# Loading the expert blocks of a routed FFN block by block instead of four at a time

## The chip, the core and the metric

The kernel runs on one core of one Trainium2 chip. The metric is the device time of one execution in microseconds. Six executions of the kernel before gave a median of 1012.49 us (1010.12 to 1017.5). One execution was profiled; its own time is 1010.9 us, and the span of the trace is 1009.1 us. Times below are microseconds from the start of that span.

## What is computed

The input is 64 sequences of 128 tokens of width 128, and a context of 77 keys of width 96 for each sequence. The reference, cut to its two steps:

```python
x = x + xattn(layernorm(x), ctx, w_q, w_kv, w_out, b_out)       # 16 heads of 64
x = x + ffn(layernorm(x), router_w, w1, w2, w3, sw1, sw2, sw3)  # 8 experts, each token goes to 2
...
for e in range(8):                     # the routed part; hidden width 176
    h = silu(x2 @ w1[e].T) * (x2 @ w3[e].T)
    moe_out = moe_out + gate[:, e:e+1] * (h @ w2[e].T)
```

A shared expert (sw1, sw2, sw3) is added for every token. The reference computes all experts for all tokens and multiplies by a gate that is zero for six of the eight; the kernel computes only the two chosen ones, except for the last tokens.

## The kernel before, in words

**Work and its order.** The 64 sequences are 16 groups of 4 (512 tokens each). The attention runs in 128 units, two for each sequence. A unit has two half slots, so the program has 256 half slots, numbered 0 to 255. Everything that is not attention is hung into half slots by hand: `at(when, step)` puts a step into the table `plan`, and `run(when)` (L979) issues the steps of one half slot in the order in which they were put there. At the end of the kernel function all instructions of one engine are tied to their program order, so every engine, and SP that issues most DMAs, works strictly in the order in which the steps were issued. There are no priorities.

**Sets and blocks.** The first 15 groups are routed in three sets of 7, 5 and 3 groups (`SETS`). For each group a router picks two experts for each token, and POOL scatters the normalised rows by indirect DMA into a DRAM buffer `sent` of the set (`send`, L587), ordered by expert. When a set is complete, `tables` (L675) counts the rows of every expert on DVE, reads eight end positions into SP's registers (`values`, L666), writes eight DMAs of filler rows (L691), and works out for each block of 128 rows where its rows begin and which expert's weights it needs. A block is 128 rows of one expert. Four blocks make a `Quad` (L725); the sets have 16, 12 and 8 quads. `Set.ready` is the half slot from which a set's quads can run: 127, 207 and 255.

**A quad's steps.** `load` (L731) reads eight table entries into SP's registers, then issues for each of the four blocks a DMA of its rows (`xb`, L740, 65 KB) and one of its packed weights (`w`, L748, 312 KB): eight DMAs, 1.5 MB. `transpose` (L751) turns the four blocks on TensorE, with a copy on ACT. `first` and `rest` are the up projections (L761) and the gate on ACT and DVE, `down` (L769) the down projection, and `answer` (L783) scatters the result by indirect DMA on POOL. A quad of the first two sets with its transposes in half slot p has `load` at p-3, `first` at p+1, `rest` at p+2 and `down` at p+4 (L900 to L909). In the first set p grows by 5 from quad to quad, in the second by 4. `xb` has 4 buffers of a whole quad; `w` has 12 buffers of one block each, so a block's weights can be loaded once the block 12 before has had its `down`.

**What else SP issues in order.** The inputs of later groups (L105, L107, L112), the attention's last values `vo` (L378, one for each sequence, right after the even half slot 4m; it waits for a buffer that the output product of two sequences before frees), the parked residuals (L616), and for the first set's results `Combine` (L795): loads of parked rows and answers (L804, L805) in half slots 211 to 223, and stores (L816) in half slots 215 to 227. A store waits for DVE's two additions (L812), which are issued one half slot earlier.

**The ending.** After half slot 255 `ending` (L957) runs a list of jobs, one pass of its loop each: the last set's quads b0 to b7 (program names 2_0 to 2_7), a shared expert, and the eight dense experts e0 to e7 for the sixteenth group. The order is b0 b1 b2 shared b3 e0 b4 e1 b5 e2 b6 e3 b7 e4 e5 e6 e7. Pass k issues: the load of job k+2; the steps of `combining` for the second set's results; `first` of job k; the transposes of job k+1; `rest` of job k; `down` and the answers of job k-1. In `combining`, passes 2 to 6 load one group's results each through POOL's queue (2 to 6 issue groups 0 to 4), and passes 4 to 8 add them on DVE (L812) and store them through SP (L816); the last set's results follow in the same way after b7. A dense expert's load is one DMA of weights (L634). The loads of b0 and b1 are issued in half slots 253 and 254, before the loop.

Of the kernel before, what the change touches and what calls it, by code (L numbers as in the profile page):

```python
# [8 lines left out]
F32 = mybir.dt.float32  # L9
# [15 lines left out]
E, I = 8, 176  # L25
# [9 lines left out]
QUAD = 4  # L35
# [15 lines left out]
DW = D + 2  # L51
# [6 lines left out]
def xattn_moe_kernel(  # L58
# [28 lines left out]
    ffn = ctx.enter_context(tc.tile_pool(name="ffn", bufs=2))  # L87
# [59 lines left out]
    rows = most * T + 128  # L147
# [57 lines left out]
    def bank(name, p=128):  # L205
        return ps_g.tile([128, 512], F32, tag="g", name=name)[:p]
# [37 lines left out]
    class Norm:  # L244


        def __init__(self, name, src):
            self.name, self.src = name, src
# [39 lines left out]
    class Attention:  # L288
# [66 lines left out]
        def values(self, b):  # L355

            vo = self.vo[b]
            for t in range(2):

                pv = bank(f"pv_{self.g}_{b}_{t}")  # L360
                for r in range(4):
                    odd, half = divmod(r, 2)
                    nc.tensor.matmul(  # L363
                        pv[r * 32 : (r + 1) * 32],
                        self.cT[:, b, 32 * half : 32 * (half + 1)],
                        wvo_sb[:, 8 * t + odd : 8 * (t + 1) : 2, :],
                        start=True,
                        stop=True,
                    )
                nc.scalar.copy(vo[:, 4 * t : 4 * (t + 1), :], pv.rearrange("p (m d) -> p m d", d=D))  # L370
# [247 lines left out]
    class Dense(Router):  # L618
# [13 lines left out]
        def load(self, e):  # L632
            self.w[e] = ffn.tile([128, WALL], F32, tag="w", name=f"w_d{e}", bufs=3 * QUAD)
            nc.sync.dma_start(out=self.w[e], in_=wx[e * 128 : (e + 1) * 128, :])  # L634
# [90 lines left out]
    class Quad:  # L725
# [2 lines left out]
        def __init__(self, st, q):  # L728
            self.st, self.q, self.name = st, q, f"{st.i}_{q}"

        def load(self):  # L731
            st = self.st
            self.w = []
            self.xb = ffn.tile([128, QUAD, DW], F32, tag="xb", name=f"xb_{self.name}", bufs=4)
            first = slice(QUAD * self.q, QUAD * (self.q + 1))
            froms = values(st.from_row[0:1, first], E * rows)
            wrows = values(st.w_row[0:1, first], (E - 1) * 128)
            for j in range(QUAD):
                w = ffn.tile([128, WALL], F32, tag="w", name=f"w_{self.name}_{j}", bufs=3 * QUAD)
                ins = nc.sync.dma_start(out=self.xb[:, j, :], in_=sent[st.i][bass.ds(froms[j], 128), :])  # L740
                for other in st.scatters:
                    tc.add_manual_dep(
                        ins.ins,
                        other.ins.name,
                        mybir.DependencyInfo(mybir.DependencyClass.Sync, mybir.DependencyReason.DATA),
                        reason="rows of this block",
                    )
                nc.sync.dma_start(out=w, in_=wx[bass.ds(wrows[j], 128), :])  # L748
                self.w.append(w)
# [73 lines left out]
    def at(when, *steps):  # L823
        plan.setdefault(when, []).extend(steps)
# [30 lines left out]
    for g in range(NG):  # L855
        p = 16 * g
# [11 lines left out]
    def route(g, step, *args):  # L868
        if g not in routers:
            st = next((s for s in sets if s.start <= g < s.start + s.n), None)  # L870
            routers[g] = (Router if st else Dense)(g, st, atts[g].x1)
        getattr(routers[g], step)(*args)
# [10 lines left out]
    for g in range(NG - 1):  # L883
        p = 16 * (g + 1)
        routing(g, p, (0, "stats"), (1, "normed"), (2, "transpose"), (3, "logits"), (4, "choose"), (5, "choose_second"))
    for st in sets:
        for g in range(st.start, st.start + st.n):
            p = 16 * (g + 1)
# [7 lines left out]
    end = 16 * NG  # L896

    for st, after in zip(sets, sets[1:]):
        until = after.ready - 4
        for q in range(st.quads):  # L900
            quad = Quad(st, q)
            p = st.ready + (until - st.ready) * q // (st.quads - 1)
            at(p - 3, quad.load)
            at(p, quad.transpose)
            at(p + 1, quad.first)
            at(p + 2, quad.rest)
            at(p + 4, quad.down)
            for j in range(QUAD):
                at(p + 5 + j // 2, lambda quad=quad, j=j: quad.answer(j))  # L909
        if after is not sets[-1]:  # L910
            for j in range(st.n):
                c = Combine(st, j, nc.sync)
                at(p + 8 + 2 * j, c.load)
                at(p + 11 + 2 * j, c.add)
                at(p + 12 + 2 * j, c.store)

    class Job:


        def __init__(self, of=None, **steps):  # L920
            self.steps = {k: getattr(of, k) for k in ("load", "transpose", "first", "rest", "down") if hasattr(of, k)}
            self.steps.update(steps)
            if of is not None:
                self.steps["answer"] = lambda: [of.answer(j) for j in range(QUAD)]

        def do(self, step):
# [11 lines left out]
    jobs = blocks[:3] + [shared]  # L938
# [18 lines left out]
    def ending():  # L957
        for k in range(max(len(jobs) + 2, max(combining) + 1)):
            job = jobs[k] if k < len(jobs) else Job()
            for step in ahead_of.get(k, ()):  # L960
                route(NG - 1, step)
            if k + 2 < len(jobs):
                jobs[k + 2].do("load")
            for step in combining.get(k, ()):
                step()
            job.do("first")
            if k + 1 < len(jobs):
                jobs[k + 1].do("transpose")
            job.do("rest")
            if 0 < k <= len(jobs):  # L970
                jobs[k - 1].do("down")
                jobs[k - 1].do("answer")

    at(end - 3, lambda: jobs[0].do("load"))
    at(end - 2, lambda: jobs[1].do("load"))
    at(end - 1, lambda: jobs[0].do("transpose"))
    at(end + 4, ending)

    def run(when):  # L979
# [124 lines left out]
```

## Time and profile before

| | |
|---|---|
| median of 6 runs | 1012.49 us |
| the profiled execution: time, span | 1010.9 us, 1009.1 us |
| TensorE (PE) | 967.0 us busy, 96%; mean granted clock 0.989 |
| VectorE (DVE) | 681.5 us, 68% |
| ScalarE (ACT) | 532.1 us, 53% |
| GpSimd (POOL) | 505.8 us, 50% |
| SP's DMA queue | 93.91 MB, its packets 30.6% of 16 engines' span |
| weights of blocks (L748) | 144 DMAs of 312 KB |
| rows of blocks (L740) | 144 DMAs of 65 KB |

How to read it. The page has for each engine its busy time, and in 40 slices how busy each was, the clock that was granted to TensorE and how busy the 16 DMA engines were. The view of waits adds up for each engine what ended its idle times. The view of windows gives the busy time of every engine, the granted clock and the DMA engines' share in stretches that the reader chooses; a share near 1 says that the transfers themselves are the limit there. The timeline of one engine lists its instructions in order with start and length; for SP these are the issues of DMAs, each about 0.33 us, not the transfers. When a transfer landed is recorded by the DMA engines' updates of its semaphore; the chain of work shows such a transfer as one piece from its issue to its landing.

### The profile page before, as it was taken

The page shows a single profiled execution, that of the slowest core. Times are in us where ns is not written, and L with a number is a line of the kernel's source. Part 1 is how long each engine was busy: PE and PEld are TensorE (multiplying, and loading weights), DVE is VectorE, ACT ScalarE, POOL GpSimd, SP SyncE. Part 2 cuts the span into 40 slices and gives each one's busy share as a digit, 9 for nine tenths or more (in the row PEclk, how much of TensorE's full clock was granted, in tenths as well). Part 3 has the DMA queues.
Part 4 walks back from the last instruction along what each step waited for, and adds up shares of the span by engine and source line. Part 5 has one row for each costly group of instructions (what it writes and reads, how often), then busy time and mean ns, then how long its engine had stood idle before and what let it go on. Part 6 is the DMA issues. An engine that isn't in the chain of part 4 may idle for free.

```text
span 1009.1 us, 19581 instructions
## 1 busy us (share of the span) xinstructions
PE 967.0 (96%) x6475; PEld 722.7 (72%) x6475; DVE 681.5 (68%) x1758; ACT 532.1 (53%) x1217; POOL 505.8 (50%) x629
## 2 busy tenths in 40 slices
PE   7999999999999997999999999999999999899896
PEld 5666667666666665768778777776777878778684
DVE  4565666677666766667656666667777866766877
ACT  4555555554646463655556565564654655445341
POOL 3334544536263625355474664646547566465542
PEclk9999999999999998999999999999999999999998
DMA  4212111211111214554343551352758575257964
GB/s 150 76 42 72 52 40 50 75 43 44 57 64 39 68 43 136 169 158 134 105 138 113 159 177 63 126 166 62 226 177 292 180 226 173 84 158 239 354 207 146
DMA packets 98372, 128.26 MB, mean 127 GB/s; under 512 B 13152, under 2 KB 62560, under 8 KB 98272
## 3 DMA queue, kind: packets, MB, share of 16 engines
q1 hardware_dynamic: 82704, 93.91, 30.6%
q0 software_dynamic: 10240, 23.73, 6.9%
q10 hardware_dynamic: 5328, 9.37, 2.5%
q8 instruction: 52, 0.85, 0.3%
q14 instruction: 48, 0.39, 0.1%
HBM read 91.23 MB, written 35.74 MB: 126 GB/s over the span
## 4 chain that ended last, share of the span: by engine, by line
PE 78%; DVE 9%; ACT 5%; DMA 3%; issue 3%; POOL 2%; ACTq 0%; DVEq 0%; SPq 0%; POOLq 0%
PE py L398 13%; PE pk L308 12%; PE ps L324 10%; PE pv L363 10%; PE p L761 5%; PE pa L388 5%; PE pq L773 3%; PE pq L774 3%; PE pn L408 3%; PE ph L761 2%; PE p_s L598 2%; PE pf L611 2%; PE pl L497 1%; PE pf L610 1%; PE pt L754 1%
## 5 line engine op out<-in xcount | busy, mean ns | idle before, releaser
L351 POOL TENSOR_TENSOR at<-sc,ri 128x512 f32<-128x512 f32 x128 | 134.6, 1052 | 267.0 <-DVE ri L348 159.0
L785 POOL DMA_INDIRECT answers<-y,to x144 | 142.2, 988 | 92.4 <-ACT y L781 37.3
L315 ACT COPY kx<-pk 128x308 f32<-128x308 f32 x256 | 100.2, 426 | 146.3 <-PE pk L308 140.1
L324 PE MATMUL ps<-kx,xgT 128*128 128x308 f32 x512 | 158.4, 431 | 10.7 <-DVE sc L335 5.8
L398 PEld LDWEIGHTS py<-vo,aT 128*128 128x128 f32 x1280 | 155.6, 195 | 12.3 <-ACT vo L370 3.8
L398 PE MATMUL py<-vo,aT 128*128 128x128 f32 x1280 | 156.6, 279 | 2.1 <-ACT vo L370 2.0
L308 PE MATMUL pk<-cT,wkq_sb 96*128 96x308 f32 x512 | 156.3, 429 | 1.0 <-DVE wkq_sb L229 1.0
L587 POOL DMA_INDIRECT sent<-pay,row x120 | 118.2, 985 | 71.3 <-DVE part L577 39.6
L339 ACT ACTIVATE sc<-sc,rs_a 128x616 f32<-128x616 f32 x128 | 105.0, 820 | 70.9 <-DVE sc L335 60.7
L346 DVE TENSOR_REDUCE sm<-sc 128x8 f32<-128x616 f32 x128 | 101.3, 791 | 50.0 <-ACT sc L339 48.4
L391 ACT COPY aT<-pa 128x512 f32<-128x512 f32 (+1 forms) x256 | 96.3, 430 | 61.4 <-PE pa L388 54.7
L363 PE MATMUL pv<-wvo_sb,cT 96*32 96x512 f32 x1024 | 123.2, 599 | 0.0
L308 PEld LDWEIGHTS pk<-cT,wkq_sb 96*128 96x128 f32 x512 | 88.8, 190 | 47.8 <-ACT aT L391 15.1
L324 PEld LDWEIGHTS ps<-kx,xgT 128*128 128x128 f32 x512 | 89.6, 191 | 46.0 <-PE pv L363 9.1
L333 DVE TENSOR_REDUCE mx<-ps 128x8 f32<-128x616 f32 x128 | 98.6, 770 | 22.0 <-PE ps L324 21.0
L335 DVE TENSOR_TENSOR sc<-ps,mx 128x616 f32<-128x616 f32 x128 | 102.3, 800 | 12.9 <-DVE mx L333 1.0
L388 PE MATMUL pa<-ident,at 128*128 128x128 f32 x640 | 91.0, 273 | 1.4 <-POOL at L351 1.3
L388 PEld LDWEIGHTS pa<-ident,at 128*128 128x128 f32 x640 | 75.7, 141 | 22.3 <-issue 11.8
L761 PEld LDWEIGHTS p<-xT,w 128*128 128x128 f32 x576 | 68.4, 192 | 9.9 <-ACT xT L756 4.0
L761 PE MATMUL p<-xT,w 128*128 128x128 f32 x576 | 71.1, 277 | 2.6 <-ACT xT L756 2.6
L370 ACT COPY vo<-pv 128x512 f32<-128x512 f32 x128 | 69.6, 587 | 1.3 <-PE pv L363 0.7
L363 PEld LDWEIGHTS pv<-wvo_sb,cT 96*32 96x32 f32 x1024 | 26.8, 109 | 48.9 <-issue 39.8
(154 smaller groups left out, 1405.8 us busy)
## 6 DMA issues: line engine op xcount, KB each, us to landing
w<-in_wx_dram SPq DMA_DIRECT2D x144, 312.0 KB
xb<-sent SPq DMA_DIRECT2D x144, 65.0 KB
last_values<-vn ACTq DMA_DIRECT2D x32, 256.0 KB
vo<-last_values SPq DMA_DIRECT2D x64, 128.0 KB
xg<-in_x_dram SPq DMA_DIRECT2D x16, 256.0 KB
xgT<-in_xT_dram SPq DMA_DIRECT2D x16, 256.0 KB
ya<-answers POOLq DMA_DIRECT2D x8, 512.0 KB, 5.9
parked<-x SPq DMA_DIRECT2D x15, 256.0 KB
```

The costliest lines, as they stand in the source:

```text
L308: nc.tensor.matmul(pk[:, :TK].rearrange("p (b k) -> p b k", k=NKV), wkq_sb[:, h, :], self.cT[:, :, :NKV], start=True, stop=True,)
L324: nc.tensor.matmul(ps[:, r, : 4 * NKV].rearrange("p (j k) -> p j k", k=NKV), self.xgT[:, ts], self.kx[:, h : h + 4, ks], start=True, stop= ...
L335: nc.vector.tensor_tensor(at, sc, over_keys(mx), ALU.subtract)
L339: nc.scalar.activation(at, at, AF.Exp, scale=self.norm.rs[:, b : b + 1])
L346: nc.vector.tensor_reduce(sm, at, AX.X, ALU.add)
L351: nc.gpsimd.tensor_tensor(main, at[:, :, :, :KM], over_keys(ri, KM), ALU.mult)
L363: nc.tensor.matmul(pv[r * 32 : (r + 1) * 32], self.cT[:, b, 32 * half : 32 * (half + 1)], wvo_sb[:, 8 * t + odd : 8 * (t + 1) : 2, :], sta ...
L388: nc.tensor.transpose(pa[:, j * NQ : (j + 1) * NQ], keys[:, c : c + 128], ident)
L398: nc.tensor.matmul(py[:, :D], aT[:, m, :], vo[:, m, :], start=(m == 0), stop=(m == NT - 1))
L587: ins = nc.gpsimd.indirect_dma_start(out=sent[st.i], out_offset=bass.IndirectOffsetOnAxis(ap=self.row[:, i : i + 1], axis=0), in_=self.pay ...
L761: nc.tensor.matmul(to[:m, ts], self.w[j][:, c : c + m], self.xT[:, ts], start=True, stop=True)
L785: ins = nc.gpsimd.indirect_dma_start(out=answers[st.i], out_offset=bass.IndirectOffsetOnAxis(ap=self.to[:, j : j + 1], axis=0), in_=self.y ...
```

## The change

`load` takes the numbers of the blocks that it is to load. The registers and the `xb` buffer are set up with block 0. In the first two sets block j is loaded in half slot p-5+j, but not before `ready`-3. In the ending a pass issues blocks 0 and 1 of job k+2 where it issued the whole load, and blocks 2 and 3 after `rest`, before the `down` of job k-1. The loads of b0 and b1 come in four half slots from 252 to 255.

```diff
-        def load(self):
+        def load(self, *js):
             st = self.st
-            self.w = []
-            self.xb = ffn.tile([128, QUAD, DW], F32, tag="xb", name=f"xb_{self.name}", bufs=4)
-            first = slice(QUAD * self.q, QUAD * (self.q + 1))
-            froms = values(st.from_row[0:1, first], E * rows)
-            wrows = values(st.w_row[0:1, first], (E - 1) * 128)
-            for j in range(QUAD):
+            if 0 in js:
+                self.xb = ffn.tile([128, QUAD, DW], F32, tag="xb", name=f"xb_{self.name}", bufs=4)
+                first = slice(QUAD * self.q, QUAD * (self.q + 1))
+                self.rows = values(st.from_row[0:1, first], E * rows), values(st.w_row[0:1, first], (E - 1) * 128)
+                self.w = []
+            froms, wrows = self.rows
+            for j in js:
...
             p = st.ready + (until - st.ready) * q // (st.quads - 1)
-            at(p - 3, quad.load)
+            for j in range(QUAD):
+                at(max(st.ready - 3, p - 5 + j), lambda quad=quad, j=j: quad.load(j))
             at(p, quad.transpose)
...
-            self.steps = {k: getattr(of, k) for k in ("load", "transpose", "first", "rest", "down") if hasattr(of, k)}
+            self.steps = {k: getattr(of, k) for k in ("transpose", "first", "rest", "down") if hasattr(of, k)}
             self.steps.update(steps)
             if of is not None:
+                self.steps["load"] = lambda: of.load(0, 1)
+                self.steps["load_more"] = lambda: of.load(2, 3)
...
             job.do("rest")
+            if k + 2 < len(jobs):
+                jobs[k + 2].do("load_more")
             if 0 < k <= len(jobs):
                 jobs[k - 1].do("down")
...
-    at(end - 3, lambda: jobs[0].do("load"))
-    at(end - 2, lambda: jobs[1].do("load"))
+    for k in range(2):
+        at(end - 4 + 2 * k, lambda k=k: jobs[k].do("load"))
+        at(end - 3 + 2 * k, lambda k=k: jobs[k].do("load_more"))
```

The number of DMAs, their sizes, the buffers, and every instruction on TensorE, DVE, ACT and POOL stay as they are; only places in SP's order change.

## Prediction

> **What bounds the kernel now.** I read the page first: engines, the 40 slices, the clock.
>
> ```profile
> PE 967.0 (96%) x6475; PEld 722.7 (72%) x6475; DVE 681.5 (68%) x1758; ACT 532.1 (53%) x1217; POOL 505.8 (50%) x629
> ...
> PE   7999999999999997999999999999999999899896
> ...
> DMA  4212111211111214554343551352758575257964
> ```
>
> TensorE is busy nearly everywhere, so a load matters only where TensorE waits for it. The DMA engines are half idle until the last slices. Next I read the view of waits of TensorE, first from 400 to 880 us (first and second set's quads), then from 912 to 972 us (the ending's quads).
>
> ```profile
> PE pr L544 <- DVE sel L541: 3.7, 3, 2.5
> PE p L761 <- ACT xT L756: 2.6, 4, 1.0
> PE ps L324 <- DVE sc L335: 1.3, 1, 1.3
> PE pq L774 <- DVE hr L465: 0.4, 1, 0.4
> PE pf L611 <- DVE hr L465: 0.3, 1, 0.3
> ```
> ```profile
> PE pt L754 <- DMA xb<-sent: 3.6, 5, 1.1
> ```
>
> The columns are total, number, longest. In 480 us TensorE waits 8.3 us, none of it for a load. All waits for rows (3.6 us) lie in the ending, 0.4 at b2 and the rest at b5's transposes, in TensorE's timeline:
>
> ```profile
> 949.56 0.30 PE L754 MATMUL pt<-ident,xb 128*128 128x128 f32 x1 [1.00 <-DMA xb<-sent]
> 950.43 0.33 PE L754 MATMUL pt<-ident,xb 128*128 128x128 f32 x1 [0.58 <-DMA xb<-sent]
> 951.86 0.33 PE L754 MATMUL pt<-ident,xb 128*128 128x128 f32 x1 [1.09 <-DMA xb<-sent]
> 952.77 0.33 PE L754 MATMUL pt<-ident,xb 128*128 128x128 f32 x1 [0.59 <-DMA xb<-sent]
> ```
>
> Four waits, 3.3 us. Windows around them show what follows (columns: length, busy time of PE, PEld, DVE, ACT, POOL, granted clock, DMA share, GB/s):
>
> ```profile
> 874.60:878.00 3.40, 1.76 (x19) 1.75 (x19) 2.84 (x13) 1.77 (x3) 1.32 (x2) 1.00 0.02 5
> 891.70:895.10 3.40, 1.42 (x13) 1.19 (x12) 1.45 (x2) 1.47 (x3) 2.92 (x5) 1.00 0.32 83
> 895.10:898.50 3.40, 3.40 (x17) 3.40 (x18) 2.36 (x5) 2.30 (x7) 0.88 (x2) 0.50 0.08 26
> 949.70:953.10 3.40, 1.15 (x5) 0.61 (x5) 3.30 (x9) 0.00 (x0) 2.20 (x4) 1.00 1.06 384
> 953.10:956.50 3.40, 3.40 (x13) 2.38 (x12) 2.42 (x5) 1.18 (x2) 0.00 (x0) 0.50 1.06 400
> ```
>
> After a stretch with TensorE busy 1.15 or 1.42 of 3.40 us the next runs at half clock, a loss of 3.4/2 = 1.7 us; after one with 1.76 busy it doesn't. So b5's wait costs 3.3 + 1.7 = 5.0 us. Pass to pass it is the same: e1's pass takes 10.56 us (946.68 to 957.24), e0's and e2's 4.80. This is **all that better loading can win**.
>
> **First and second set.** Nothing is added but SP's order. I compared for every quad the landing of its last rows with its transposes. From the second quad of the first set to its last, and in the second set except for its first quad (2.4) and quads 1_3 to 1_6 (4.0 to 7.5), rows lie ready 14 us or more; the reason is that SP runs ahead. Half slot p-3 hides behind two gates: `vo` of 4m waits for an output product that is issued some four half slots earlier, and the weights for `down` of three quads before. Blocks 0 to 2 keep these gates, so five half slots ahead buys little. A half slot lasts 3.7 us here (quads 1_3 and 1_4, four half slots apart, transpose at 769.4 and 784.3). The places with little cover are these.
>
> (a) The last quad of a set: `tables` of the next set stands in half slots 201 and 249, where block 3 of quads 0_15 and 1_11 now comes too, behind it. Filler DMAs end at 697.75 and 890.35, so block 3's rows are issued at 697.9 and 890.5 instead of 666.0 and 864.8. Unloaded rows take 1.8 us (395.3 to 397.1): landed 699.8 and 892.3, or 0.8 later behind eight fillers. The fourth transposes want them at 699.9 and 892.6, so up to 0.8 us is lost each. But TensorE idles right behind both, 1.30 us for DVE at 700.2 and 1.98 us for ACT at 893.0. I take 0, and 1.6 if that cover goes.
>
> (b) Quads 1_3 and 1_4: block 3 moves to 217 and 221, behind a store and loads of 768 KB. Those are issued at 765.0 and 779.5; rows behind them land near 769 and 783, transposes are at 769.7 and 784.7. I take 0; with landings 2 us later, 1.7 and 0.3.
>
> (c) First quads: block 3 goes behind one `vo`, 0.5 us; rows are ready 2.4 and 3.1 us early. 0. For b0 and b1 the gate is the scattered rows of their set (issue at 897.5), not the half slot; `vo` now behind b0's first half is issued near 899.6 and wanted at 909.6. 0.
>
> **The ending.** Here SP's order bites. The store of pass k now stands between the halves of job k+2's load: passes 4, 6 and 8, that is b4, b5 and b6. It waits for DVE's additions.
>
> ```profile
> 932.27 0.36 SPq L740 DMA_DIRECT2D xb<-sent  x1
> 932.86 0.33 SPq L748 DMA_DIRECT2D w<-in_wx_dram  x1
> 936.56 0.41 SPq L816 DMA_DIRECT2D out_dram<-ya  x1
> 937.07 0.44 SPq L634 DMA_DIRECT2D w_d<-in_wx_dram  x1
> 942.16 0.40 SPq L816 DMA_DIRECT2D out_dram<-ya  x1
> 943.51 0.34 SPq L740 DMA_DIRECT2D xb<-sent  x1
> ...
> 947.17 0.33 SPq L740 DMA_DIRECT2D xb<-sent  x1
> ```
>
> *b4.* Its last rows were issued at 932.27, landed at 937.4; transposes 938.76 to 939.2. Now they come behind the store of 936.56: 937.07 and three steps of some 0.5 give 938.6. The DMA engines are full (share 1.00 at 366 GB/s from 932 to 942), and landings follow the order of issue. That store landed at 941.39 with b4's second half before it, 0.77 MB or 2.1 us; without it 939.3. Two blocks' rows and one block's weights (0.45 MB) add 1.2, answers in between 0.4: 940.9. Loss 1.8 us; bounds: unloaded 938.6 + 1.8 = 940.4, so 1.2; as slow as b5's last rows (947.17 to 952.73, 5.55 us) 944.2, so 5.0. I take 1.8, since the queue ahead is known.
>
> *b5.* b5's first half still waits for the store of 942.16, so nothing comes earlier. Its rows lie behind 1.5 MB of Combine's loads (issued on POOL 941.2 to 942.9, landed by 949.1); the second half gets one more store ahead, 0.26 MB or 0.7 us at 366 GB/s: 953.4 instead of 952.73. The additions before that store wait for Combine's loads (946.2), not for TensorE, so b4's 1.8 us is swallowed here: TensorE arrives at b5's transposes later and waits less. Together b4 and b5 cost **0.7 us**, not 2.5. The clock may go either way: a shorter wait can leave the window above 1.76 us busy and give back 1.7.
>
> *b6.* Rows move behind the store of 959.41, to 961.0; landing takes 1.8 to 4.0 us there (958.25 to 962.25), so 962.8 to 965.0 against a fourth transpose at 963.7. Loss 0 to 1.3; I take 0.3, the nearer to b6's other rows. b7 and the rest have no store ahead.
>
> **Sum.** 0 + 0.7 + 0.3 = +1.0 us on the profiled 1009.1, with +1.6 and +2.0 if (a) and (b) lose their cover and -1.7 if the clock stays up. Time outside the span is 1.8 us (1010.9), unchanged: 1011.9. The median of the runs lies 1.6 above the profiled one: **1013.5**.
>
> The Trainium skill, "TensorE: Matmul & The Clock Gate", section "HAM oscillation", asks for no TensorE gap above about 3.4 us. The rows above differ: the clock fell after gaps of 1.98 and of 1.09 us at most. By the page b4's wait could never cost a clock step; by the rows it could.
> The skill's "DMA: Bandwidth & Descriptors", section "Queues, rings and completion order", says that each engine alternates between queues packet by packet. Then b5's first rows (0.33 MB with the store ahead, at half of 366 GB/s: 1.8 us, plus an unloaded 1.8) would land at 947.1, not at 949.42 as recorded, and the split would bring b5's wait down by some 2 us: estimate 1011.5. I go by the recorded landings.
>
> **Rivals.**
> *Slower: second halves late three times.* Place: the stores of passes 4, 6 and 8. If full DMA engines give each second half the 5.55 us of b5's last rows, b4's transposes end at 944.4, the gate of e0 and the additions behind it on DVE near 949, b5's last rows are issued at 951 and land at 956.5, 3.8 later than now (b4's loss is swallowed in that); b6 adds up to 1.3. Total 3.8 to 5.1: 1017. It decides from the point where b5's last rows land more than 3 us later than now. For: every store waits for DVE in order, and the share is above 1. Against: same bytes, and known queues.
> *Faster: b5's wait goes.* Fewer loads at once let b5's rows through in time: -3.3 - 1.7 = -5.0, 1007.5. For: it is the only wait for rows, and the chain of waits runs through it. Against: its first issue stays at the store of 942.
> *In the middle: (a) and (b) lose their cover*, +3.6 at most, 1016 with the sum; likelier half of it, 1014.5, within the bound.
> *No spreading at all:* the gates, not the half slots, set the issues. Same time; part of my forecast.
>
> **Numbers.** 0.3%, about what a measurement of this kernel can tell from no change, is 3.0 us. Forecast 0.40, the middle 0.08 more, both within; slower 0.30; faster 0.22. The range reaches to both outer cases: 1007 to 1017.5.
>
> **What would show it.** Right: b4's transposes wait 1 to 3 us, b5's less than before, its last rows land near 953.4; no wait for rows of quads 1_3 or 1_4 above 1 us. Wrong: b5's wait is gone (faster), or b5 and b6 wait longer with half-clock windows behind (slower), or quads in the middle wait for rows.

## The result, and the profile after

The changed kernel takes 1017.15 us (median of 20 runs, 1012.47 to 1022.54); the kernel before, beside it, 1012.69 us (45 runs). The ratio is **1.0045**, 95% interval 1.0033 to 1.0057: slower by 4.5 us. The forecast was +1.0 us. The profiled execution took 1016.22 us with a span of 1014.5 us, 5.4 us more than the span before. All times below are microseconds from the start of the span of the trace that is spoken of.

The page, the same lines as before:

```profile
PE 970.9 (96%) x6475; PEld 726.1 (72%) x6475; DVE 681.1 (67%) x1758; ACT 532.2 (52%) x1217; POOL 505.4 (50%) x629
...
PE   7999999999999997999999999999999999999896
...
DMA  4211111211121215535244353423848764276954
```

TensorE is busy 3.9 us longer with the same 6475 instructions, so some of them ran slower; the slices are too coarse to show where. All half-clock stretches together are as long as before (24.3 and 24.0 us), but more of them lie where TensorE has work. The rows' lines in the views of TensorE's waits, from 400 to 880 us and from 920 to 985 us:

```profile
PE pt L756 <- DMA xb<-sent: 1.2, 1, 1.2
```
```profile
PE pt L756 <- DMA xb<-sent: 5.5, 5, 1.9
```

In the middle there is one wait for rows (quad 0_15); in the ending b4, b5 and b6 wait 5.5 us together, where b5 alone waited 3.3. (Quad 1_11 and b2 wait between the two views; they are in the table below.) TensorE's timeline shows which:

```profile
942.38 0.33 PE L756 MATMUL pt<-ident,xb 128*128 128x128 f32 x1 [1.86 <-DMA xb<-sent]
943.58 0.33 PE L756 MATMUL pt<-ident,xb 128*128 128x128 f32 x1 [0.87 <-DMA xb<-sent]
...
954.98 0.33 PE L756 MATMUL pt<-ident,xb 128*128 128x128 f32 x1 [0.31 <-DMA xb<-sent]
...
965.95 0.33 PE L756 MATMUL pt<-ident,xb 128*128 128x128 f32 x1 [1.61 <-DMA xb<-sent]
967.10 0.33 PE L756 MATMUL pt<-ident,xb 128*128 128x128 f32 x1 [0.81 <-DMA xb<-sent]
```

b4 waits 2.73 us, b5 0.31, b6 2.42, always for blocks of the second half of the load. Behind b4 and behind b6 the clock falls, behind b5 it doesn't; two windows of b4, one of b5, two of b6 (columns as in the prediction: length, busy time of PE, PEld, DVE, ACT, POOL, granted clock, DMA share, GB/s):

```profile
941.00:944.40 3.40, 1.15 (x4) 0.68 (x5) 3.13 (x5) 0.46 (x1) 3.08 (x5) 1.00 0.99 330
944.40:947.90 3.50, 3.50 (x16) 3.15 (x15) 1.53 (x3) 0.72 (x2) 0.00 (x0) 0.51 1.04 378
953.00:956.40 3.40, 3.09 (x14) 1.60 (x13) 3.26 (x8) 1.37 (x3) 2.10 (x3) 1.00 0.98 334
964.90:968.30 3.40, 1.53 (x6) 0.86 (x7) 2.69 (x7) 0.58 (x1) 0.00 (x0) 1.00 0.99 322
968.30:971.70 3.40, 3.40 (x18) 3.40 (x18) 1.53 (x3) 0.71 (x2) 0.00 (x0) 0.50 0.97 286
```

**Where the 5.4 us come from.** I matched the matmuls of the two traces one by one and took start after minus start before:

| reached | after minus before | what happened in between |
|---|---|---|
| 397 us | -0.96 | half clock ahead of the first quad lasts 3.4 us, not 6.8 |
| quad 0_15 done | -0.96 | waits 1.18 us for block 3, all of it regained |
| 880 us | +0.69 | one half-clock stretch at 876.2 |
| quad 1_11 done | +0.41 | waits 1.26 us, regained |
| 899 us | -1.22 | the half-clock stretch of 895.1 is gone |
| after b2 | +1.38 | b2 waits 0.99 instead of 0.39; half clock at 924.0 |
| after b4 | +6.18 | waits 2.73, half clock at 944.4 |
| after b5 | +0.56 | waits 0.31 instead of 3.3; the half clock of 953.1 is gone |
| after b6 | +5.05 | waits 2.42, half clock at 968.3 |
| last matmul | +5.43 | |

All that stays is from b2 on. b4 and b5 cancel: 4.8 lost, 5.6 regained. b6, the last quad with a store between its halves, loses 4.5 us that nothing gives back. b2 loses 2.6, most of it by the half clock at 924.0, and that need not come from a late load: it follows TensorE's wait of 1.27 us for the router (`pl`, L497), which the kernel before has too, and three kernels below in which b2 waits for nothing (e6, e8, e9) have half clock at the same place (924.1, 923.9, 923.8).

**Why b6 is late.** SP's timeline of the changed kernel, the last issue of b6's first half, the store of pass 8 and the first of the second half:

```profile
959.26 0.33 SPq L750 DMA_DIRECT2D w<-in_wx_dram  x1
962.27 0.40 SPq L818 DMA_DIRECT2D out_dram<-ya  x1
962.86 0.36 SPq L742 DMA_DIRECT2D xb<-sent  x1
```

SP stands 2.7 us at that store. The stores of passes 7 and 8 in the kernel before:

```profile
953.13 0.39 SPq L816 DMA_DIRECT2D out_dram<-ya  x1
...
959.41 0.40 SPq L816 DMA_DIRECT2D out_dram<-ya  x1
```

So the store of pass 8 is 2.9 us later, and that of pass 7, ahead of b6's first half, comes at 955.42 for 953.13. TensorE, though, is only 0.6 us later at b6 than before, as b5 paid b4's loss back. The chain of waits says what holds that store (start, length, what):

```profile
953.12 0.95 POOL answers L787
954.08 5.40 DMA ya<-parked
...
960.83 0.70 DVE ya L814
...
962.27 0.40 SPq L818
963.98 3.07 DMA xb<-sent
```

Read it from below: b6's rows behind the store, the store behind the additions, these behind the load of group 4's results, and that load behind b3's answers in POOL's order. b3's answers come from `down` of b3, which TensorE does right behind b4's transposes. So the first theory was: **b4's wait goes down POOL, DVE and SP and comes up again at b6, although TensorE has been paid back at b5.** The rival: b6's second half is late by its own place.

### The profile page after: what moved, and what is told of

Same layout as the page of the kernel before. It is cut to its first block, busy times and chain, and to the rows that moved or that the text cites. A ratio compares the mean times of both kernels' runs of the same rounds, so it can differ in the third digit from the quotient of the medians.

```text
span 1014.5 us, 19568 instructions
## 1 busy us (share of the span) xinstructions
PE 970.9 (96%) x6475; PEld 726.1 (72%) x6475; DVE 681.1 (67%) x1758; ACT 532.2 (52%) x1217; POOL 505.4 (50%) x629
## 5 line engine op out<-in xcount | busy, mean ns | idle before, releaser
L398 PEld LDWEIGHTS py<-vo,aT 128*128 128x128 f32 x1280 | 153.2, 193 | 10.5 <-ACT vo L370 1.9
L398 PE MATMUL py<-vo,aT 128*128 128x128 f32 x1280 | 154.2, 276 | 0.3 <-ACT vo L370 0.2
```

What stands on the lines that cost most here:

```text
L398: nc.tensor.matmul(py[:, :D], aT[:, m, :], vo[:, m, :], start=(m == 0), stop=(m == NT - 1))
```

## The experiments

Runs of one group share one chip and its runs of the kernel before. In the first group (e1 to e4) the kernel before itself takes 1044.68 us (26 runs), so ratios are compared, not microseconds. The second (e5 to e8) and third (e9 to e12) had 1013.4 and 1012.93 us (35 runs each). The record gives chip 12 for the first and the third group and chip 1 for the second, so what made the first one slow is not known; in the traces of e1, e2 and e3 TensorE is already 18 to 20 us behind at 690 us, long ahead of the ending.

**e1, only the spreading in the sets.** The ending as before:

```diff
-                self.steps["load"] = lambda: of.load(0, 1)
-                self.steps["load_more"] = lambda: of.load(2, 3)
+                self.steps["load"] = lambda: of.load(0, 1, 2, 3)
```

> Only the first two sets' quads are loaded block by block; the ending and its first two loads are as before. Theory (the stores between the halves in the ending make the loss): within 1 us of before, 1012 to 1014; TensorE waits about 1.2 us for the fourth rows of quads 0_15 and 1_11, and stands no later behind them than before. Rival 1 (late rows in the middle cost the time): 1015.5 to 1017.

Measured: 1050.31 us, ratio 1.0076 (1.0047 to 1.0106, 6 runs). This spoke for the rival, so it was run again (e11).

**e2, only the halves in the ending.** The sets as before:

```diff
-            for j in range(QUAD):
-                at(max(st.ready - 3, p - 5 + j), lambda quad=quad, j=j: quad.load(j))
+            at(p - 3, lambda quad=quad: quad.load(0, 1, 2, 3))
```

> Only the ending (and the four half slots ahead of it) loads in halves; the first two sets load four blocks at once as before. Theory: the whole loss, 1016 to 1018, with waits for rows at b4 and b6 (2 to 3 us each) and a half-clock window behind each. Rival 1: 1012 to 1014.

Measured: 1050.48 us, ratio 1.0071 (1.0044 to 1.0098). Its waits in the ending:

```profile
PE pt L756 <- DMA xb<-sent: 7.9, 4, 2.7
```

In the timeline these are 2.67 and 1.39 at b4 and 2.06 and 1.76 at b6; b5 waits for nothing. That is the pattern of the changed kernel without the sets' part.

**e3, the halves, with the store behind the second one.** As e2, and:

```diff
-        combining.setdefault(k + n, []).append(step)
+        (storing if step.__name__ == "store" else combining).setdefault(k + n, []).append(step)
...
                 jobs[k + 2].do("load_more")
+            for step in storing.get(k, ()):
+                step()
```

> As the run with the ending alone, but the store of a pass is issued behind the second half of the load instead of ahead of it; nothing else moves. Theory: the waits at b4 and b6 go, 1011 to 1013.5, b5 still waits. Rival 2 (the DMA engines are full, and loading in halves later in the pass is what hurts, wherever the store stands): 1015 to 1018.

Measured: 1044.14 us, ratio 0.9999 (0.9982 to 1.0017). Its waits in the ending:

```profile
PE pt L756 <- DMA xb<-sent: 3.2, 4, 1.3
```

All four are b5's; b4 and b6 wait for nothing. The same halves at the same places of the pass, with only the store moved, cost nothing. So the store between the halves is the place, as the prediction had it. The ratios alone would be weaker evidence: e1, in the same group, was as slow as e2 without any halves in the ending. It is the waits, 4.1 us at b4 and 3.8 at b6 that go with the store, that set e2 and e3 apart.

**e4, each half one half earlier.** A pass issues the second half of job k+2 and the first of job k+3, both ahead of its store:

```diff
     def ending():
+        jobs[2].do("load")
...
             if k + 2 < len(jobs):
-                jobs[k + 2].do("load")
+                jobs[k + 2].do("load_more")
+            if k + 3 < len(jobs):
+                jobs[k + 3].do("load")
...
             job.do("rest")
-            if k + 2 < len(jobs):
-                jobs[k + 2].do("load_more")
```

> The ending loads in halves that both stand ahead of the pass's store, the first half of job k+3 and the second of job k+2, so half of every quad comes one pass earlier than before; the sets are as before. Theory (what binds b5 is the place of its load behind the store of pass 5): b5's wait of 3.3 us and the half-clock window behind it shrink or go, 1008 to 1011.5. Rival 2 (full DMA engines bind b5): 1012 to 1014.

Measured: 1042.2 us, ratio 0.9978 (0.9955 to 1.0000), the only one that could be faster than the kernel before; run again as e12.

**e5, one quad's load in halves, all others whole; and e6, another.** The test of the theory of b6:

```diff
+                late = of.name == f"{len(SETS) - 1}_3"
+                self.steps["load"] = lambda: of.load(*((0, 1) if late else range(QUAD)))
```

> The sets' quads are loaded as in the kernel before, and so are all quads of the ending but b4 (2_4), whose load goes in two halves with the store of pass 4 between them. Theory (the store stands between the halves, and a late b4 makes b6 late by way of its answers, the loads of the results, the additions and the store that SP then waits for): the last transposes of b4 wait 2 to 3 us as in the changed kernel, b5, whose load is whole and ahead of the store, waits no more than in the kernel before (3.3 us) less what b4 took, the additions of group 4 come about as late as in the changed kernel; the sum is 1 to 4 us, a ratio of 1.001 to 1.004 to the kernel before on the same chip. Rival (each half is late at its own place only, and what b4 loses b5 gets back): no difference, 0.999 to 1.001.

> All quads are loaded as in the kernel before but b6 (2_6), whose load goes in two halves with the store of pass 6 or 8 between them. Theory (b6 was late in the changed kernel because b4 had been late before it, through the answers and the additions of group 4): the store comes as early as in the kernel before, b6's last transposes wait at most 0.8 us, no window at half clock follows, a ratio of 0.999 to 1.001 to the kernel before. Rival (the second half of b6 is late by its own place, whatever b4 did): its transposes wait about 2.4 us and a window at half clock of 3.4 us follows, 3 to 5 us, a ratio of 1.003 to 1.005.

The edits missed what the expectations speak of: the number is the quad's, and 3 and 5 (in e6) are b3 and b5, not b4 and b6. They tell something else. e5, 1013.27 us, ratio 1.0002 (0.9988 to 1.0016): b3 has no store between its halves, and its rows lie ready 4.0 us early as in the kernel before; the cut alone is free. e6, 1014.3 us, 1.0009 (0.9996 to 1.0022): b5 alone in halves waits 5.5 us, where it waits 2.6 to 4.2 in the traces that load b4 and b5 whole (before, e5, e8, e10, e11). So its store costs waiting as well, as long as TensorE doesn't come late to it.

**e9, b4 alone in halves.** As e5, with `_4`.

> The two kernels meant for b4 and b6 split the loads of 2_3 and 2_5 instead; here it is 2_4. All other quads are loaded as in the kernel before. Theory (a late b4 is paid back by b5, and comes again at b6 by way of the answers, the loads of the results, the additions and the store of pass 8): the last transposes of b4 wait 2 to 3 us, b5's less than 1 us where they waited 2.9 to 3.3, b6, whole and ahead of that store, none; the additions of group 4 come late against their place in the kernel before, as in the changed kernel. Ratio to the kernel before 0.999 to 1.002. Rival (b4's wait is not paid back): b5 waits as long as in the kernel before, and the ratio is 1.002 to 1.004.

Measured: 1013.17 us, ratio **0.9996** (0.9985 to 1.0008). TensorE's timeline, a wait of b4 and those of b6:

```profile
942.86 0.33 PE L756 MATMUL pt<-ident,xb 128*128 128x128 f32 x1 [1.82 <-DMA xb<-sent]
...
964.61 0.33 PE L756 MATMUL pt<-ident,xb 128*128 128x128 f32 x1 [0.47 <-DMA xb<-sent]
965.79 0.33 PE L756 MATMUL pt<-ident,xb 128*128 128x128 f32 x1 [0.85 <-DMA xb<-sent]
```

b4 waits 2.5 us (0.66 more at its fourth block), b5 doesn't wait at all, and b6, whole and ahead of its store, waits 1.3 us, which it does not in the kernel before. SP's timeline, the store of pass 7 and b6's first rows, says why:

```profile
955.74 0.40 SPq L818 DMA_DIRECT2D out_dram<-ya  x1
957.53 0.34 SPq L742 DMA_DIRECT2D xb<-sent  x1
```

The stores of passes 7 and 8 are at 955.74 and 962.74, as in the changed kernel (955.42, 962.27), with POOL's load of group 4's results at 954.25 (954.08 there, 951.05 before); so b6's whole load begins at 957.53 instead of 954.75. The theory expected no wait at b6 here; it has one, smaller, since the store of pass 7 is late too. That store is not held by POOL's loads (group 3's results landed at 949.1 before and at 951.4 here, ahead of need) but by DVE's order: its additions stand behind b4's gate and e0's sums (L655), which follow TensorE, and begin at 954.31 for 951.70 before. The ratio shows that b4's loss is repaid: b4 + b5 + b6 wait 3.8 us here and 3.3 before.

**e10, b6 alone in halves.**

> All quads loaded as in the kernel before but b6 (2_6), in two halves with the store of pass 8 between them. Theory (b6 was late in the changed kernel since b4 had been late): b6's last transposes wait at most 0.8 us, no window at half clock follows, a ratio of 0.999 to 1.001 to the kernel before. Rival (the second half of b6 is late by its own place): its transposes wait 1.5 to 2.5 us and a window at half clock of 3.4 us follows, 3 to 5 us, a ratio of 1.003 to 1.005.

Measured: 1013.22 us, ratio **1.0005** (0.9993 to 1.0017). b6's transposes on TensorE, and the store of pass 8 on SP:

```profile
967.71 0.85 PE L756 MATMUL pt<-ident,xb 128*128 128x128 f32 x4
```
```profile
963.63 0.40 SPq L818 DMA_DIRECT2D out_dram<-ya  x1
```

The store stands between the halves here as well, but this whole ending runs some 4 us later than in the kernel before (b4's transposes begin at 942.70 for 938.76, b6's at 967.71 for 963.40), so 963.63 is about the store's old place (959.41 + 4.2). The four transposes take 0.85 us, without a named wait, where undisturbed ones take 0.60 in these traces: at most 0.3 us is lost and no half clock follows. The rival (b6 by its own place) falls. b6's wait by the two edits, in us, each number from one execution:

| | b6 whole | b6 in halves |
|---|---|---|
| b4 whole | 0 (before, e5, e6, e8, e11) | at most 0.3 (e10) |
| b4 in halves | 1.3 (e9) | 2.4 (changed kernel), 1.7 (e7, the same again), 3.8 (e2) |

**e7, the changed kernel again; e8, the sets with block 3 beside block 2 in p-3; e11, e1 again.**

```diff
-                at(max(st.ready - 3, p - 5 + j), lambda quad=quad, j=j: quad.load(j))
+                at(max(st.ready - 3, p - 5 + min(j, 2)), lambda quad=quad, j=j: quad.load(j))
```

> The changed kernel itself once more, beside the others on one chip. If the parts add up as the first four runs have them (blocks of the sets one by one 1.0076, halves in the ending 1.0071), the ratio to the kernel before is 1.010 to 1.015 on a chip like that of those runs; by the first comparison it is 1.0045. Theory (the loss is in the ending alone): 1.003 to 1.008 on every chip, and the loss in the quads of the sets was of those few executions. Rival (both parts cost): over 1.010 on a chip like that one.

> The ending as in the kernel before; in the sets block j is loaded in half slot p-5+j, but block 3 together with block 2 in p-3, so that no block is loaded later than in the kernel before and none of the last quads' blocks stands behind the tables of the next set. Theory (what the sets' part costs, if anything, is the last block behind the tables): a ratio of 0.998 to 1.002 to the kernel before. Rival (blocks issued earlier cost by themselves, since SP waits longer for buffers ahead of other loads): 1.004 to 1.008 as with all four blocks apart.

> The blocks of the first two sets one by one, the ending as before, a second time. Theory (the loss is in the ending): a ratio of 0.999 to 1.002 to the kernel before, about that of the version that keeps block 3 ahead of the tables. Rival (the quads of the sets cost by themselves): the 1.0076 of the first such run, or 1.004 and more.

e7: 1016.81 us, ratio 1.0025 (1.0008 to 1.0042); b4 waits 2.57, b5 0.59, b6 1.69 us, and b2, ahead of them, 2.65. By the same matching as above b6 costs 2.1 us in this trace (no half clock follows it) and b2 6.2 (half clock at 919.3 and 926.2). e8: 1014.12 us, 1.0014 (1.0001 to 1.0027). e11: 1013.47 us, **1.0000** (0.9985 to 1.0016). In these two groups the sets' part costs nothing that can be measured, and keeping block 3 ahead of `tables` gains nothing. The 1.0076 of e1 did not come back. The groups are not alike: e1's trace shows half clock at 455.1, 523.4, 646.3, 902.3 and 919.3, where the kernel before at 1010.9 us has none between 397 and 895. But e3, with a ratio of 0.9999, has such stretches at nearly the same places (454.9, 523.2, 649.5, 902.1, 919.1), so they belong to the group and not to the sets' part. What the sets' part does there stays open: e1's profiled execution is the fastest of its six, and holds no loss to be read.

**e12, e4 again.**

> The ending with the second half of job k+2 and the first half of job k+3 ahead of the stores of pass k, the sets as before, a second time, on another chip if one is given. Theory (what the ending of the kernel before loses, 3.3 us of wait at b5 and up to 1.7 us of half clock behind it, is a load that comes too late): 0.994 to 0.998. Rival (the loads are bound by their buffers or by the DMA engines, so earlier places bring nothing): 0.999 to 1.001.

Measured: 1011.93 us, ratio 0.9995 (0.9980 to 1.0010). Not faster; the theory of a gain falls. SP's timeline, the store of pass 5 and the rows of b5's third block:

```profile
945.29 0.41 SPq L818 DMA_DIRECT2D out_dram<-ya  x1
945.90 0.35 SPq L742 DMA_DIRECT2D xb<-sent  x1
```

The first half is earlier (issued at 941.76 and 942.86, rows landed at 945.1 and 946.4, before 949.4 and 950.4), but the second stands behind the store of pass 5, is issued where it was (945.90 and 947.01; 946.07 and 947.17 before), and lands at 952.3 and 953.3, 6.3 us after its issue (before 951.8 and 952.7). b5's wait falls to 0.98 us only since TensorE comes later, after 1.6 us at b2 and half clock at 919.4. No version here is shown to beat the kernel before.

**Do the parts add up?** In the second and third group: sets 1.0000, b3 1.0002, b4 0.9996, b5 1.0009, b6 1.0005; together 1.0012, with some 0.0012 to 0.0016 of uncertainty in each. The whole change measured 1.0025 (1.0008 to 1.0042) and 1.0045 (1.0033 to 1.0057), so the first is not clear of the sum. What is over fits the combination, b4 late and b6 cut, which the table above shows in waits; b4 and b6 in halves with all others whole was not run, so its price in time is argued, not shown. Nor were b0 to b2 in halves run alone. b2 waits 1.0 and 2.65 us in the two traces of the changed kernel and 0 to 2.1 where it is loaded whole, so a share of the loss may lie there. All halves of the ending without the sets' part were run in the slow first group alone.

## Why the prediction was partly right

**What bounds, and where the change can act: right.** Only b2 to b6 moved the end; the ending's store between the halves is the place (e2 against e3). One reading was loose: the passes that are to show the same 5.0 us differ by 10.56 - 4.80 = 5.76.

**(a) Last quads behind the tables: right, sizes off.** Block 3 was issued at 697.0 and 891.2 (forecast 697.9 and 890.5) and landed at 700.3 and 894.8, 3.3 and 3.6 us later, not 1.8 to 2.6. The waits are 1.18 and 1.26 us, not up to 0.8; the idle time behind them took both, as the table of shifts shows.

**(b), (c): right.** Rows of quads 1_3 and 1_4 lie ready 2.2 and 0.6 us before their transposes; b0 and b1 don't wait.

**b4: mechanism right, size off.** Forecast 1.8 us (bounds 1.2 to 5.0), measured 2.73. The second half was issued from 938.51 to 939.63 (forecast up to 938.6, and TensorE was 1.4 later by then); its last rows took 3.9 us, not 2.3.

**b5 swallows b4: right, and better than forecast.** Together +0.7 forecast; the waits are 2.73 + 0.31 against 3.3 before, -0.2. b5's last rows landed at 954.9, for a forecast of 953.4. Its first rows landed 6.4 us after their issue (944.29 to 950.72), not 3.6 as in the estimate of 1011.5, so the recorded landings were the better guide.

**b6: the step that failed.** "Rows move behind the store of 959.41 ... I take 0.3." The place and the size are those of a kernel in which b4 is on time: e10 measured at most 0.3. The store itself moved to 962.27. I had followed b4's loss along TensorE only, where b5 repays it, and not along POOL, DVE and SP, where nothing repays it. Measured 2.42 us, and with the half clock behind it TensorE lost 4.5 (2.1 in e7).

**The clock: the second error.** I took 0, with -1.7 as the other end. The half clock of b5 went, and the new waits of b4 and b6 were followed by one each (944.4, 968.3): 1.7 us more from the loads. The third new stretch of the ending, at 924.0, is none of theirs (e6, e8 and e9 have it too) and costs another 1.7 in this trace. That b4's wait could cost a clock step was read rightly: its longest gap was 1.86 us. A new wait need not bring one: behind b6's 1.69 us in e7 the clock stayed up.

**The rivals.** The slower case gave 1017, the measured time, but not by its mechanism: it was to decide from b5's last rows landing over 3 us later, and they landed 2.2 later with b5's wait nearly gone. That its number was met is luck. It named passes 4, 6 and 8, and the middle one cost nothing in this order. The faster case had b5's wait gone, which happened, and the time was lost before and behind it.

## What to carry to other kernels

An instruction queued in order between two halves of a load makes the second half as late as whatever that instruction waits for; cut a load only where nothing that waits stands at the cut, or put the store behind both halves. A delay that the bounding engine gets back at its next wait is not gone: follow it down every other engine's queue until it has no consumer left. And where a wait goes because the engine arrives later, no time is won.

## What the runs showed of the hardware

**A stretch at half clock needs no idle window, and its place is a matter of phase.** The half-clock stretches begin whole multiples of some 3.41 us apart: 924.0, 944.4 and 968.3 are 6 and 7 of them apart. The same 2.5 us wait of `pr` (L544) was cut in two by that grid in the kernel before (TensorE busy 1.76 us of 874.6 to 878.0; the clock stayed at 1.00), and fell into one piece in the changed one (0.92 of 872.8 to 876.2, half clock from 876.2):

```profile
872.80:876.20 3.40, 0.92 (x12) 0.92 (x12) 2.81 (x9) 0.97 (x2) 1.38 (x2) 1.00 0.01 2
876.20:879.60 3.40, 3.40 (x17) 3.27 (x16) 2.08 (x11) 1.87 (x7) 1.97 (x2) 0.50 0.09 24
...
920.60:924.00 3.40, 2.13 (x19) 1.92 (x18) 1.36 (x5) 2.10 (x7) 1.52 (x2) 0.99 0.94 289
924.00:927.40 3.40, 3.40 (x19) 3.40 (x18) 1.38 (x2) 0.68 (x2) 2.79 (x4) 0.50 0.50 167
```

The last pair shows that the busy share of the profile doesn't decide alone: 2.13 us busy, and half clock follows. In e7 a stretch with 1.71 busy was followed by full clock:

```profile
967.10:970.50 3.40, 1.71 (x8) 0.84 (x7) 2.82 (x7) 0.59 (x1) 0.12 (x1) 1.00 0.91 285
970.50:973.90 3.40, 3.40 (x32) 3.40 (x31) 1.53 (x3) 2.03 (x6) 0.25 (x1) 1.00 0.96 313
```

What decides stays open. The Trainium skill, "TensorE: Matmul & The Clock Gate", section "Part 1: The HAM clock gate (the "warmup" mystery)", says that the activity window runs freely, 3413 ns each, and doesn't start with the kernel; the spacing above agrees. It gives half clock after at least one idle window; the stretches above were partly busy (0.92 to 2.13 of 3.40), so here the measurement decides.

**b2's wait varies though its load stays the same.** With b2 loaded whole, in the same place of SP's order, it was 0.4 (before), 0 (e6, e8, e9), 1.0 (e5), 1.5 (e11) and 2.1 us (e10). Such waits can be part of why single executions of one kernel lie some 8 us apart, which no run here takes apart; a single profile doesn't settle a difference of 0.1 or 0.2%.
